# The seam between a scan layer and an attention layer: the last half's output made inside the attention, its matrices folded beside the scan, the last product in four blocks

## The chip, the cores and the metric

The kernel runs on one core of a Trainium2 chip. The metric is the device time of one execution in microseconds (us). Five engines take part, each with its own queue of instructions that it works through in order: TensorE (PE; its weight loads are shown apart as PEld), VectorE (DVE), ScalarE (ACT), GpSimd (POOL) and SyncE (SP), which here only issues DMA transfers. Engines wait for each other by semaphores.

## What is computed

Four images of 32 x 32 positions with 256 channels (4096 rows of 256 numbers, float32) go through two layers. Cut to what matters here:

```python
# layer 0: normalize, project to 512, 3x3 depthwise convolution, gelu, then for every
# batch, channel d and state n (64 of them) a recurrence over the 1024 positions:
h = exp(dt[:, :, None] * A) * h + (dt * x)[:, :, None] * B[:, None, :]
y = einsum('bdn,bn->bd', h, C)
y = layernorm(y + x * D_skip) * g + b
t = src + y @ w_out + b_out
# layer 1: an attention without softmax over the positions of one batch
qkv = layernorm(t) @ W_qkv + b_qkv
q, k = q - mean(q), k - mean(k)          # over channels
k2 = l2norm(k*k / (sum(k*k) + 1e-7), over positions)
q2 = l2norm(q*q / (sum(q*q) + 1e-7), over channels)
t = t + (v + q2 @ (k2^T v) / sqrt(N)) @ W_out + b_out
# then a mixture of 16 experts, two of them for each row
t = t + experts(layernorm(t))
```

The means of q and k over the channels, and the product of v's weights with W_out, depend on the weights alone. The kernel folds them into the weights: it takes off the column means and the row means of W_qkv and multiplies the v part by W_out.

## The kernel before, in words

**The scan.** The recurrence runs over eight units, (batch, half): a half is 512 positions. A unit has 64 states, and a state has four blocks of 128 channels, so a unit has 256 slots. In each slot ScalarE makes one `da` (decay, L695) and one `bx` (scale, L687), PE turns bx (turn, L701), VectorE scans 512 positions (scan, L712). After a state's fourth block POOL multiplies the whole state by C (L719, 128 x 2048), and PE adds the product up, turned, into four PSUM banks y0 to y3 (add_up, L733), nine slots late (LAG). The C row of a state is fetched by SP three states ahead (fetch, L681, four buffers). When a unit is over, close_sum (L746) copies the four banks to `ysb`, two on VectorE and two on ScalarE.

The order of the scan is written out by hand: the loop at L815 walks the slots. Other work is slipped in beside it: `beside(u)` (L753) lists what is due in unit u, as pieces with an engine, a cost and a window of slots; a piece is put in when its slot has come, its gap has passed, its engine has room in the slot (MOST) and, for PE, the single spare bank `bg` is free. In this way the convolution of a later unit, its projections (dt_bc) and the output of the unit before (after_stats, roots_after, after) run beside the scan. In the last two units there is no convolution left to make.

**The output of a unit** (after, L587): per 128 rows, x's rows are fetched (`xr`), b_out is added on POOL, ysb is turned on PE and copied to `yT`, multiplied by w_o (L616), scaled by the row's root and added to xr, and stored in DRAM in `td` (L627). For the last unit nothing is left to hide it beside: it runs alone after the scan (L866 to L871), with its roots made by a logarithm, an exponential and a correction on POOL.

**The attention** (from L925) is not ordered by hand: a scheduler orders each engine's queue when the program is built. It first loads W_qkv, W_out and the biases, and the four batches' rows `t_all` from td (L941, 1 MB each). Then it folds the weights (L945 to L1004): sums by a matmul with ones (L953), means taken off (L958 to L977), v's weights turned and multiplied by W_out (L983 to L994), biases likewise. The loop over the batches (L1018) takes row statistics (statistics, L1006: BN and aggregate on VectorE, a root on ScalarE, a reciprocal), scales the rows to `xh` on ScalarE (L1023), turns them to xhT on PE (L120, copied by VectorE at L1027), and for each of 8 tiles of 128 rows multiplies by the q and k weights (`pqk`, L1037), adds the bias (`qk`, L1042), squares and sums, and multiplies by the folded v weights (`pv`, L1054). The rest of a batch, the routing and the experts (L1326 on) follow.

Of the kernel before, what the change touches and what calls it, by code (L numbers as in the profile page):

```python
# [16 lines left out]
P = 128  # L17
# [16 lines left out]
def conv_ssm_attn_moe_kernel(ctx: ExitStack, tc: tile.TileContext, a: dict, out: bass.AP):  # L34
# [99 lines left out]

    with ExitStack() as l0:
# [3 lines left out]
        scanp = l0.enter_context(tc.tile_pool(name="scan", bufs=2))  # L139
        ps_y = l0.enter_context(tc.tile_pool(name="ps_y", bufs=1, space=PSUM))  # L140
        ps_w = l0.enter_context(tc.tile_pool(name="ps_w", bufs=3, space=PSUM))
# [38 lines left out]
        w_o = load_rows("L0_conv_w_out", DK, C, w0)  # L180
        b_o = load_bcast("L0_conv_b_out", C, w0)
# [33 lines left out]
        for m in range(DK):  # L215
            pad = w0.tile([P, HH + 2, WW + 2], F32, name=f"pad{m}")
            nc.gpsimd.memset(pad, 0.0)
            pads.append(pad)
# [426 lines left out]

        def run(*lists):
            for todo in lists:
                for _, _, _, what, _, _ in todo:
                    what()
# [54 lines left out]
        def scan(s, m):  # L704
            u, n = steps[s]
            b, seg = units[u]
            if m == 0:
                made["h", s] = scanp.tile([P, DK, BANK + 1], F32, name="h", bufs=4)
            if seg == 0 and n == 0 and m == 0:
                last[b] = acts.tile([P, NS, DK], F32, name="last", bufs=1)  # L710
            h = made["h", s]
            nc.vector.tensor_tensor_scan(  # L712
                h[:, m, 1:], made.pop(("da", s, m)), made.pop(("dbx", s, m)),
                0.0 if seg == 0 else last[b][:, n, m : m + 1],
                ALU.mult, ALU.add,
            )
            if m == DK - 1:

                nc.gpsimd.tensor_tensor(  # L719
                    h[:, :, :BANK], h[:, :, 1:], over_middle(made["c", s], DK), ALU.mult  # L720
                )
                if seg + 1 < NHALF:
                    with nc.allow_non_contiguous_dma(reason="one element a partition"):
                        nc.sync.dma_start(out=last[b][:, n, :], in_=h[:, :, BANK])
# [21 lines left out]
        def close_sum(u):  # L746
            t = acts.tile([P, TPB, DN], F32, name="ysb", bufs=1)
            for j in range(TPB):
                eng = nc.scalar.copy if j % 2 else nc.vector.tensor_copy
                eng(t[:, j, :], made["y", u][j])  # L750
            made["ysb", u] = t

        def beside(u):  # L753
# [8 lines left out]
            if v < n:  # L762
                b, half = units[v]
                if u == 0:
                    lists.append([
                        (head(b, 0), (11, 44)), (head(b, 1), (44, 77)), (conv(v), (77, 236)),
                    ])
                elif half == 0:
                    lists.append([(head(b, 1), HEAD1), (conv(v), CONV0)])
                else:  # L770
                    lists.append([(conv(v), CONV1)])
                    if b + 1 < NB:
                        lists[-1].append((head(b + 1, 0), HEAD0))
            if u > 0:
                lists.append([(after_stats(u - 1), STATS)])
# [22 lines left out]
        AFTER = ((14, 110), (112, 245))  # L798

# [66 lines left out]
        alone = True  # L866
        u = len(units) - 1
        run(after_stats(u))
        logs(made["rs"], made["mv"][:, :, 1])
        roots_after(u)  # L870
        run(*after(u, None))  # L871

# [52 lines left out]
    with tc.tile_pool(name="wa", bufs=1) as wa, tc.tile_pool(name="att", bufs=1) as att, \  # L925
            tc.tile_pool(name="sm", bufs=2) as sm, \
            tc.tile_pool(name="ps_b", bufs=2, space=PSUM) as ps_b:
        wqkv = load_rows("L1_attn_W_qkv", CK, 3 * C, wa)
        bqkv = load_bcast("L1_attn_b_qkv", 3 * C, wa)
        bv = load_column("L1_attn_b_qkv", CK, wa, lo=2 * C)  # L930
        wout = load_rows("L1_attn_W_out", CK, C, wa)
        bout = load_bcast("L1_attn_b_out", C, wa)
# [6 lines left out]
        tbs = [t_all[:, b * NT : (b + 1) * NT, :] for b in range(NB)]  # L939
        for b in range(NB):  # L940
            nc.sync.dma_start(out=tbs[b], in_=rows(td, b))  # L941

        wcat = wa.tile([P, CK, 3 * C], F32, name="wcat")  # L945
        wv = wa.tile([P, CK, C], F32, name="wv")
        bcat = wa.tile([P, 3 * C], F32, name="bcat")
        every1 = wa.tile([P, P], F32, name="every1")
        nc.vector.memset(every1, 1.0)
        for n0, n in ((0, 2 * C), (2 * C, C)):  # L950
            ps = ps_b.tile([P, BANK], F32, name="pw", tag="pq", bufs=3)
            for ck in range(CK):
                nc.tensor.matmul(  # L953
                    ps[:, :n], every1, wqkv[:, ck, n0 : n0 + n],
                    start=(ck == 0), stop=(ck == CK - 1),
                )
            for ck in range(CK):
                nc.vector.scalar_tensor_tensor(  # L958
                    wv[:, ck, :] if n0 else wcat[:, ck, :n], ps[:, :n], -1.0 / C,
                    wqkv[:, ck, n0 : n0 + n], ALU.mult, ALU.add,  # L960
                )
        mean = sm.tile([P, CK, 2], F32, name="w_mean")
        for ck in range(CK):
            qk = wcat[:, ck, : 2 * C].rearrange("p (s c) -> p s c", s=2)
            nc.vector.tensor_reduce(mean[:, ck, :], qk, AX.X, ALU.add)
            for s in range(2):
                nc.vector.scalar_tensor_tensor(
                    qk[:, s, :], mean[:, ck, s : s + 1].to_broadcast([P, C]), -1.0 / C,
                    qk[:, s, :], ALU.mult, ALU.add,
                )  # L970
        bmean = sm.tile([P, 2], F32, name="b_mean")
        bqk = bqkv[:, : 2 * C].rearrange("p (s c) -> p s c", s=2)
        nc.vector.tensor_reduce(bmean, bqk, AX.X, ALU.add)
        for s in range(2):
            nc.vector.scalar_tensor_tensor(
                bcat[:, s * C : (s + 1) * C], bmean[:, s : s + 1].to_broadcast([P, C]), -1.0 / C,
                bqk[:, s, :], ALU.mult, ALU.add,  # L977
            )
        wvT = wa.tile([P, CK, C], F32, name="wvT")
        for m in range(CK):  # L980
            ps = ps_b.tile([P, BANK], F32, name="pw", tag="pq", bufs=3)
            for ck in range(CK):
                nc.tensor.transpose(  # L983
                    ps[:, blk(ck, P)], wv[:, ck, blk(m, P)], ident
                )
            nc.scalar.copy(wvT[:, m, :], ps[:, :C])
        for ck in range(CK):
            ps = ps_b.tile([P, BANK], F32, name="pw", tag="pq", bufs=3)
            for m in range(CK):
                nc.tensor.matmul(  # L990
                    ps[:, :C], wvT[:, m, blk(ck, P)], wout[:, m, :],
                    start=(m == 0), stop=(m == CK - 1),
                )
            nc.scalar.copy(wcat[:, ck, 2 * C :], ps[:, :C])  # L994
        bvw = wa.tile([P, CK, P], F32, name="bvw")
        nc.vector.tensor_copy(bvw, over_last(bv, P))
        ps = ps_b.tile([P, BANK], F32, name="pw", tag="pq", bufs=3)
        for m in range(CK):
            nc.tensor.matmul(
                ps[:, :C], bvw[:, m, :], wout[:, m, :], start=(m == 0), stop=(m == CK - 1)  # L1000
            )
        bvo = wa.tile([P, C], F32, name="bvo")
        nc.vector.tensor_copy(bvo, ps[:, :C])
        nc.gpsimd.tensor_tensor(bcat[:, 2 * C :], bvo, bout, ALU.add)  # L1004

        def statistics(tb, tag):  # L1006

            mv = sm.tile([P, NT, 2], F32, name="ln_mv", tag=tag + "mv")
            for i in range(NT):
                st = sm.tile([P, 6], F32, name="ln_st", tag=tag + "st")  # L1010
                nc.vector.bn_stats(st, tb[:, i, :])
                nc.vector.bn_aggr(mv[:, i, :], st)
            rs = sm.tile([P, NT], F32, name="ln_rs", tag=tag + "rs")
# [3 lines left out]

        for b in range(NB):  # L1018
            tb = tbs[b]
            _, rs = statistics(tb, "ln2")  # L1020
            xh = att.tile([P, NT, C], F32, name="xh", bufs=2)
# [12 lines left out]
            for i in range(NT):  # L1034
                pqk = ps_b.tile([P, 2, C], F32, name="pqk", tag="pq", bufs=3)
                for ck in range(CK):
                    nc.tensor.matmul(  # L1037
                        pqk.rearrange("p s c -> p (s c)"), xhT[:, ck, blk(i, P)],
                        wcat[:, ck, : 2 * C], start=(ck == 0), stop=(ck == CK - 1),
# [3 lines left out]
                    qk, pqk, bcat[:, : 2 * C].rearrange("p (s c) -> p s c", s=2), ALU.add  # L1043
# [7 lines left out]
                nc.gpsimd.tensor_tensor(tb[:, i, :], tb[:, i, :], bcat[:, 2 * C :], ALU.add)  # L1051
                pv = ps_b.tile([P, C], F32, name="pv", tag="pq", bufs=3)
                for ck in range(CK):
                    nc.tensor.matmul(  # L1054
                        pv, xhT[:, ck, blk(i, P)], wcat[:, ck, 2 * C :],
# [61 lines left out]
            for ck in range(CK):  # L1117
                pw = ps_b.tile([P, C], F32, name="pkw", tag="po")
                for m in range(CK):
                    nc.tensor.matmul(  # L1120
                        pw, kvT[:, m, blk(ck, P)], wcat[:, m, 2 * C :],
# [355 lines left out]
```

## Time and profile before

| | |
|---|---|
| time, median of 3 runs | 3609.48 us (3608.98 to 3614.11) |
| profiled execution | 3609.15 us |
| its span, first to last instruction | 3607.3 us |
| busy share PE, VectorE, ScalarE, POOL | 90%, 83%, 79%, 69% |
| chain that ended last: ScalarE, PE | 60%, 20% |
| end of the last scan | 2796.5 us |
| first product of the experts | 3141.3 us |

The span stands 1.85 us below the time of the same execution. In the profile, a group row gives line, engine, operation, output and inputs by the program's names, shapes and count, then busy time, the mean of one in ns, and the idle time of that engine just before them with what ended it. A timeline row gives start and length in us, then the same names; in brackets stands how long the engine had been idle and who released it. A row of the waits gives who waited for whom, the sum in us, how often, and the longest.

The units of the scan end (first copy of ysb) at 471.6, 811.9, 1148.2, 1488.5, 1825.1, 2162.3, 2490.6 and 2802.6 us. In the unit from 2162.3 to 2490.6, VectorE is busy for 315.1 us and ScalarE for 326.2; in the last one, to 2802.5, for 303.4 and 302.3.

### The profile page before, as it was taken

How to read it: one execution, taken by the hardware profiler on the slowest of the kernel's cores; microseconds unless marked ns; L12 is line 12 of the kernel's file. 1: busy time of each engine (PE TensorE's matmuls, PEld its weight loads, DVE VectorE, ACT ScalarE, POOL GpSimd, SP SyncE). 2: the span in 40 equal slices, each digit the busy share in tenths (PEclk: the TensorE clock that was granted, in tenths of full speed). 3: DMA queues.
4: the chain of work that ended last, by engine and by line, in shares of the span. 5: the costliest groups of instructions: out<-in, count | busy, mean ns of one | idle time of the engine just before them, and what ended most of it. 6: DMA issues, size and time to landing. Idle time of an engine off the chain costs nothing.

```text
span 3607.3 us, 60573 instructions
## 1 busy us (share of the span) xinstructions
PE 3245.6 (90%) x22292; PEld 2626.9 (73%) x22292; DVE 2981.9 (83%) x3398; ACT 2863.8 (79%) x4748; POOL 2484.2 (69%) x906
## 2 busy tenths in 40 slices
PE   8989999999998998999999989898999788599995
PEld 3678777777777777777777777777777455399985
DVE  5799999999999999999999999999999666622224
ACT  1799999999999999999999999999999244121211
POOL 0489878987897798879878987998888110033331
PEclk9999999999999999999999999999999999699997
DMA  3223222212222122222222122222121200299996
GB/s 101 64 55 76 56 64 65 61 57 58 71 69 60 62 62 61 64 63 66 60 64 64 57 59 54 55 58 57 55 60 55 73 24 12 100 381 325 319 302 236
DMA packets 355165, 334.41 MB, mean 93 GB/s; under 512 B 162081, under 2 KB 241441, under 8 KB 354866
## 3 DMA queue, kind: packets, MB, share of 16 engines
q1 hardware_dynamic: 334834, 306.21, 29.1%
q0 software_dynamic: 7104, 19.41, 1.6%
q10 hardware_dynamic: 12928, 4.89, 0.5%
q8 instruction: 177, 2.90, 0.3%
q14 instruction: 122, 1.00, 0.1%
HBM read 304.21 MB, written 25.69 MB: 91 GB/s over the span
## 4 chain that ended last, share of the span: by engine, by line
ACT 60%; PE 20%; DMA 8%; DVE 7%; issue 2%; POOL 0%; POOLq 0%; DVEq 0%; ACTq 0%; SPq 0%
ACT da L695 28%; ACT bx L687 28%; DMA yd<-yb,dst 6%; PE ps L701 4%; PE y L733 3%; PE p L1377 3%; DVE h L712 3%; PE pqk L1037 2%; PE bg L382 1%; PE pf L1389 1%; DMA xb<-xd,src 1%; PE pv L1054 1%; PE ps L382 1%; PE ps_t L120 1%; ACT L695 1%
## 5 line engine op out<-in xcount | busy, mean ns | idle before, releaser
L719 POOL TENSOR_TENSOR h<-h,cb_n 128x2048 f32<-128x2048 f32 x512 | 2143.6, 4192 | 416.7 <-DVE h L712 328.0
L701 PE MATMUL ps<-ident,bx 128*128 128x128 f32 x8192 | 1323.3, 283 | 197.8 <-DVE h L712 138.0
L687 ACT ACTIVATE bx<-dtxT,bT 128x512 f32<-128x512 f32 x2048 | 1451.5, 709 | 16.5 <-DVE dtxT L534 16.5
L695 ACT ACTIVATE da<-dt,l_conv_a_log_sb 128x512 f32<-128x512 f32 x2048 | 1452.2, 709 | 13.6 <-DVE h L712 13.3
L701 PEld LDWEIGHTS ps<-ident,bx 128*128 128x128 f32 x8192 | 937.2, 142 | 632.8 <-DVE h L712 307.9
L712 DVE TENSOR_TENSOR_SCAN h<-da,last,ps 128x512 f32<-128x512 f32 x1024 | 1231.6, 1263 | 30.3 <-ACT da L695 21.6
L733 PE MATMUL y<-ident,h 128*128 128x128 f32 x8192 | 1246.1, 275 | 5.7 <-POOL h L719 5.6
L712 DVE TENSOR_TENSOR_SCAN h<-da,ps 128x512 f32<-128x512 f32 x1024 | 1189.5, 1207 | 49.4 <-ACT da L695 32.6
L733 PEld LDWEIGHTS y<-ident,h 128*128 128x128 f32 x8192 | 974.5, 143 | 7.8 <-POOL h L719 6.7
L1383 DVE TENSOR_TENSOR hT<-s,p 128x256 f32<-128x256 f32 x148 | 62.4, 421 | 336.4 <-ACT s L1382 336.4
L1377 PE MATMUL p<-xT,w 128*128 128x128 f32 x2368 | 291.6, 277 | 0.5 <-ACT xT L1366 0.5
L1377 PEld LDWEIGHTS p<-xT,w 128*128 128x128 f32 x2368 | 285.1, 194 | 4.8 <-ACT xT L1366 0.9
L1382 ACT ACTIVATE s<-p 128x256 f32<-128x256 f32 x148 | 56.9, 384 | 275.5 <-PE p L1377 275.5
L1397 POOL DMA_INDIRECT yd<-yb,dst x74 | 73.2, 990 | 264.5 <-DMA yd<-yb,dst 185.9
L382 PE MATMUL bg<-pad,dgc 128*128 128x512 f32 x432 | 222.2, 596 | 0.0
L1346 POOL DMA_INDIRECT xb<-xd,src x74 | 72.1, 975 | 132.8 <-DVE dst L1318 108.7
L1389 PE MATMUL pf<-w,hT 128*128 128x256 f32 x592 | 153.3, 382 | 0.1
L1051 POOL TENSOR_TENSOR t_all<-t_all,bcat 128x256 f32<-128x256 f32 x32 | 23.0, 747 | 164.6 <-ACT xh L1023 159.9
L1389 PEld LDWEIGHTS pf<-w,hT 128*128 128x128 f32 x592 | 101.7, 192 | 8.2 <-DVE hT L1383 0.5
L1366 ACT COPY xT<-px 128x256 f32<-128x256 f32 x74 | 27.6, 372 | 77.5 <-PE px L1364 77.5
L382 PEld LDWEIGHTS bg<-pad,dgc 128*128 128x128 f32 x432 | 65.5, 192 | 0.0
L382 PE MATMUL ps<-pad,dgc 128*128 128x512 f32 x144 | 64.0, 605 | 0.7 <-DVE e L487 0.7
(287 smaller groups left out, 2056.5 us busy)
## 6 DMA issues: line engine op xcount, KB each, us to landing
cb_n<-cd SPq DMA_DIRECT2D x512, 256.0 KB, 3.3
w<-in_L_ffn_w_dram SPq DMA_DIRECT2D x222, 512.0 KB, 6.2
dgc<-diags SPq DMA_DIRECT2D x84, 192.0 KB, 3.1
y<-yd SPq DMA_DIRECT2D x8, 1024.0 KB, 9.6
last<-h SPq DMA_DIRECT2D x256, 2.0 KB, 2.9
xr<-in_x_dram SPq DMA_DIRECT2D x32, 128.0 KB, 3.2
td<-xr SPq DMA_DIRECT2D x32, 128.0 KB, 3.3
t_all<-td SPq DMA_DIRECT2D x4, 1024.0 KB, 10.0
```

The source lines that it names most:

```text
L382: nc.tensor.matmul(made["bg"].rearrange("p (h w) -> p h w", w=WW), made["dgc", m * 3 + i][:, j, :], pads[m][:, half * ROWS + i : (half + 1 ...
L687: nc.scalar.activation(t, made["dtxT", u][:, j, :], AF.Copy, scale=made["bT", u][:, j, n : n + 1])
L695: nc.scalar.activation(t, made["dt", u][:, m, :], AF.Exp, scale=A[:, m, n : n + 1])
L701: nc.tensor.transpose(t[:, blk(j, P)], made["bx", s, j][:, blk(m, P)], ident)
L712: nc.vector.tensor_tensor_scan(h[:, m, 1:], made.pop(("da", s, m)), made.pop(("dbx", s, m)), 0.0 if seg == 0 else last[b][:, n, m : m + 1] ...
L719: nc.gpsimd.tensor_tensor(h[:, :, :BANK], h[:, :, 1:], over_middle(made["c", s], DK), ALU.mult)
L733: nc.tensor.matmul(made["y", u][j][:, blk(m, P)], made["h", s][:, m, blk(j, P)], ident, is_transpose=True, start=n == 0 and m == 0, stop=n ...
L1037: nc.tensor.matmul(pqk.rearrange("p s c -> p (s c)"), xhT[:, ck, blk(i, P)], wcat[:, ck, : 2 * C], start=(ck == 0), stop=(ck == CK - 1),)
L1346: nc.gpsimd.indirect_dma_start(t, None, xd[:, :], bass.IndirectOffsetOnAxis(src[:, i : i + 1], 0))
L1377: nc.tensor.matmul(p12[:, j, s, :], on[w, i][:, ck, blk(h + j, P)], on["xT", i][:, ck, :], start=(ck == 0), stop=(ck == CK - 1),)
L1389: nc.tensor.matmul(on["pf", i], on["hT", i][:, hk, :], on["w3", i][:, hk, :], start=(hk == 0), stop=(hk == HK - 1),)
L1397: nc.gpsimd.indirect_dma_start(yd[:, :], bass.IndirectOffsetOnAxis(dst[:, i : i + 1], 0), yb, None)
```

## The change

Five parts:

- The folding of the attention's weights moves from the attention to the scan: `matrices()` is a list of pieces that `beside` puts into the second-to-last unit (u = 6), in slots 20 to 245. The results lie in the memory of the convolution's padded images, which are no longer needed there; a new pool, keep0, holds these, w_o, b_o and ysb beyond layer 0. The six loads that belong to it are issued by SP.
- In the last state of the last unit, POOL multiplies each block of 128 channels by C as soon as it is scanned, in four instructions of 128 x 512 in place of one of 128 x 2048.
- The block that made the last unit's output after the scan is gone. `last_half()` makes it inside the attention, behind the first batch's statistics, with the attention's own `statistics` for the roots, and adds it to x's rows in place in t_all. It is not stored in td.
- The first batch's rows are fetched first, in two halves; x's rows of the last half follow. `load_rest` fetches the other batches' rows after the first batch's reciprocal: VectorE writes one element of each place first, so that the loads wait for it.
- The PSUM pools ps_w and ps_y change places.

```diff
+    keep0 = ctx.enter_context(tc.tile_pool(name="keep0", bufs=1))
+    w_o = keep0.tile([P, DK, C], F32, name="l0_conv_w_out_sb")
+    b_o = keep0.tile([P, C], F32, name="l0_conv_b_out_row")
...
+        ps_w = l0.enter_context(tc.tile_pool(name="ps_w", bufs=3, space=PSUM))
         ps_y = l0.enter_context(tc.tile_pool(name="ps_y", bufs=1, space=PSUM))
-        ps_w = l0.enter_context(tc.tile_pool(name="ps_w", bufs=3, space=PSUM))
...
+            def load():
+                nc.sync.dma_start(out=wqk, in_=w_in[:, :, : 2 * C])
+                nc.sync.dma_start(out=wv, in_=w_in[:, :, 2 * C :])
+                nc.sync.dma_start(
+                    out=wout, in_=a["L1_attn_W_out"].rearrange("(k p) n -> p k n", p=P)
+                )
+                nc.sync.dma_start(out=bqk, in_=b_in[: 2 * C].partition_broadcast(P))
+                nc.sync.dma_start(out=bout, in_=a["L1_attn_b_out"].partition_broadcast(P))
...
+            todo = [
+                piece(1, "SP", 0, load),
+                piece(1, "DVE", 0.2, lambda: nc.vector.memset(ones1, 1.0)),
+            ]
+            for w, n in ((wqk, 2 * C), (wv, C)):
+                for ck in range(CK):
+                    todo.append(piece(
+                        8 if ck == 0 else 1, "PE", 0.88 * n / BANK,
+                        lambda w=w, n=n, ck=ck: sums(w, n, ck), "" if ck else "take",
+                    ))
+                for ck in range(CK):
+                    todo.append(piece(
+                        1 if ck else 3, "DVE", 0.69,
+                        lambda w=w, n=n, ck=ck: off_columns(w, n, ck), "free" if ck else "",
+                    ))
+            for w, m in ((wqk[:, 0, :], mean[:, 0, :]), (wqk[:, 1, :], mean[:, 1, :]), (bqk, bmean)):
+                todo.append(piece(1, "DVE", 0.69, lambda w=w, m=m: rows_of(w, m)))
+                for s in range(2):
+                    todo.append(piece(1, "DVE", 0.42, lambda w=w, m=m, s=s: off_rows(w, m, s)))
...
+            if s == len(steps) - 1:
+                nc.gpsimd.tensor_tensor(h[:, m, :BANK], h[:, m, 1:], made["c", s], ALU.mult)
+            elif m == DK - 1:
-            if m == DK - 1:
...
+            if v == n:
+                lists.append([(matrices(), MATS)])
...
-        alone = True
-        u = len(units) - 1
-        run(after_stats(u))
-        logs(made["rs"], made["mv"][:, :, 1])
-        roots_after(u)
-        run(*after(u, None))
...
+        tbs = [t_all[:, b * NT : (b + 1) * NT, :] for b in range(NB)]
+        for g in range(NHALF):
+            nc.sync.dma_start(
+                out=tbs[0][:, blk(g, TPB), :], in_=rows(td, 0)[:, blk(g, TPB), :]
+            )
+        nc.sync.dma_start(out=tbs[-1][:, TPB:, :], in_=rows(xf, NB - 1)[:, TPB:, :])
+
+        def load_rest(rs):
+            for b in range(1, NB):
+                n = TPB if b == NB - 1 else NT
+                t = tbs[b][:, :n, :]
+                nc.vector.tensor_copy(t[:, :1, :1], rs[:, :1])
+                nc.sync.dma_start(out=t, in_=rows(td, b)[:, :n, :])
...
+        def last_half():
+            ysb = made["ysb", len(units) - 1]
+            _, rs = statistics(ysb, "ln1", TPB)
+            for j in range(TPB):
+                t = tbs[-1][:, TPB + j, :]
+                nc.gpsimd.tensor_tensor(t, t, b_o, ALU.add)
+                ps = ps_b.tile([P, BANK], F32, name="ps_l", tag="po")
+                for m in range(DK):
+                    nc.tensor.transpose(ps[:, blk(m, P)], ysb[:, j, blk(m, P)], ident)
+                yT = sm.tile([P, BANK], F32, name="yT")
+                nc.vector.tensor_copy(yT, ps)
+                po = ps_b.tile([P, C], F32, name="po_l", tag="po")
+                for m in range(DK):
+                    nc.tensor.matmul(
+                        po, yT[:, blk(m, P)], w_o[:, m, :], start=(m == 0), stop=(m == DK - 1)
+                    )
+                nc.vector.scalar_tensor_tensor(
+                    t, po, rs[:, j : j + 1], t, ALU.mult, ALU.add
+                )
...
         for b in range(NB):
             tb = tbs[b]
             _, rs = statistics(tb, "ln2")
+            if b == 0:
+                load_rest(rs)
+                last_half()
```

## The prediction

> **What bounds the kernel now.** I read the page first, then the timeline of the seam between the scan and the attention, then the waits of single stretches. On the page, the shares of the chain and the groups say that the scan (28% + 28% on ScalarE) is set by ScalarE's bx and da activations, and that VectorE's scan stands close behind.
>
> ```profile
> span 3607.3 us, 60573 instructions
> ...
> L695 ACT ACTIVATE da<-dt,l_conv_a_log_sb 128x512 f32<-128x512 f32 x2048 | 1452.2, 709 | 13.6 <-DVE h L712 13.3
> L712 DVE TENSOR_TENSOR_SCAN h<-da,last,ps 128x512 f32<-128x512 f32 x1024 | 1231.6, 1263 | 30.3 <-ACT da L695 21.6
> ```
>
> The change touches the scan's last two units and what follows. The timeline of that seam (start, length, what, idle before it and who ended it):
>
> ```profile
> 2796.65 4.17 POOL L719 TENSOR_TENSOR h<-h,cb_n 128x2048 f32<-128x2048 f32 x1 [0.51 <-POOL h L719]
> ...
> 2802.55 1.29 DVE L750 COPY ysb<-y 128x512 f32<-128x512 f32 x2 [6.03 <-PE y L733]
> ...
> 2812.65 3.45 PE L616 MATMUL ps<-l_conv_w_out_sb,yT 128*128 128x256 f32 x8 [2.80 <-DVE yT L610]
> ...
> 2826.86 5.64 SPq L941 DMA_DIRECT2D t_all<-td  x4
> 2826.98 4.36 PE L953 MATMUL pw<-l_attn_w_qkv_sb,every 128*128 128x512 f32 x8 [4.21 <-issue]
> ...
> 2839.25 1.28 ACT L1014 ACT_TABLE_LOAD   x1 [3.53 <-DVE ln_mv L1012]
> ...
> 2841.56 3.31 ACT L1023 ACTIVATE xh<-t_all,ln_rs 128x256 f32<-128x256 f32 x8 [0.72 <-issue]
> ...
> 2848.87 0.69 DVE L1042 TENSOR_TENSOR qk<-pqk,bcat 128x512 f32<-128x512 f32 x1 [0.17 <-PE pqk L1037]
> ```
>
> The reader is to see a serial road: the last scan ends at 2796.5, the last product (POOL) at 2800.8, the sums are copied out at 2802.6, then the last half's output is made and stored (to 2823.7), weights are loaded and folded (2820 to 2837), t_all is fetched (2826.9), and only at 2841.56 does batch 0 start. From the scan's end to the first qk it is 52.4 us, in which no engine is full. From there PE repeats 2.58 us per tile (the eight qk rows run from 2848.87 to 2866.93).
>
> Waits in the scan's second-to-last unit (2162 to 2491 us), where new work goes:
>
> ```profile
> DVE h L712 <- ACT da L695: 7.9, 4, 3.3
> ...
> ACT da L695 <- DVE h L712: 2.0, 3, 0.7
> ```
>
> ScalarE waits there for VectorE only three times, 2.0 us in all. Pairing each da row with its scan row shows where: VectorE falls up to 7.0 us behind around slots 40 to 55 of 256, catches up at the long activations near slot 90, and is within 0.1 us of ScalarE after that.
>
> [...] 2048 elements take 4192 ns, but 512 (L518, sum_up) take 1276 ns, so four of these are 5.1 us and not 4.2. [...] the trace has 1.28 us, on the road at 2839.25. [...] Here the eight L616 instructions after an idle stretch took 3.45 us, and 1.99 us once warm (2817.55). [...] the four 1 MB loads of t_all landed about 5.5 us after the first issue and then 3.0 us apart.
>
> **The change part by part.** Time is counted as in the trace; T = 2796.5 is the last scan's end. The built order (which fixes each queue and what each wait is for) was read for the rest.
>
> *Preparing the matrices beside the scan* (matrices, MATS) takes the fold off the road. Its instructions stand in unit 6. VectorE gets 0.17 (memset, as L949) + four off_columns (2 x 0.65, 2 x 0.37, from L958: 1.29 and 0.74 a pair) + three reductions (0.63 each, L965) + six off_rows (0.36 each, L967) + two copies of 512 (0.67), bvw 0.30, bvo 0.42: 8.3 us. PE gets about 6 us in a unit that has 299 of 328 busy; POOL one 0.73; SP six loads, 1.4 MB, some 0.4 us of issue each, between C fetches that run three states, 14.7 us, ahead. ScalarE gets nothing. VectorE's part costs only where ScalarE is already held up: in the built order the memset and two off_columns of wqk, 1.5 us, lie at slots 29 to 47, at the peak of the lag; two of 0.37 at slots 72 and 73, where the lag is 3.3 us and has room; the other 6 us come after slot 98, one piece in 8 slots or so, where the lag is 0.1 us and VectorE needs 1.17 against ScalarE's 1.225 a slot. Bounds: 0 (hidden by the 7.9 us for which VectorE waits) and 8.3. I take +1.3.
>
> *Last state's products block by block.* The POOL product before ends at 2796.1. Four blocks at 1.276 end at 2801.3, 0.5 later than the single one; but PE then has 4 matmuls left instead of 16, and the copy needs only the first. From 2800.83 to 2802.55 it was 1.72; now about 0.45. ysb starts at 2801.75, a gain of 0.8. Bounds: 1.3 (blocks at a quarter of 4.19) and 0.4.
>
> *Batch 0's rows alone.* In the built order its two 512 KB loads follow the last C fetch on SP and wait only for the last scan: issue at 2796.6, landed [...] by 2800.3 and 2801.9. x's 512 KB (for the last half) follow, by 2803.4. All are in before VectorE is free at 2803.0 (two ysb copies, 1.29).
>
> *Batch 0's statistics.* Eight tiles at 0.43 (two BN and two aggregates every 0.87 from 2838.36 on), and the built order puts two of ysb's at about 0.70 among them: 4.9 us, to 2807.9. Then table load, root, reciprocal as before, 2.31 us (2839.25 to 2841.56): xh at 2810.3. VectorE's other ysb statistics and the first yT copy, 2.1 us, lie under this. Before it was 2841.56: **31.3 us earlier**.
>
> *Last half's output inside batch 0.* This gives part back. What goes: stores to td and reloads of that half, the Ln and Exp tables, POOL's refinement. SP loses four stores and four loads, two of which stood between the last C fetches; POOL's four t + b_o (0.73 each) wait for x's rows and end by 2806.4, before batch 0 needs POOL. What comes in between xh and the first qk: on PE four transposed groups (0.5) and four groups of L616's kind, the first cold (3.4, as at 2812.65), then 1.99; on VectorE four yT copies (0.67) and four additions (0.48), each waiting for PE and PE for it. PE's queue in the built order: out 0, turn 1, eight transposes of xh (ck = 0), out 1, turn 2, the other eight, out 2, turn 3, half of pqk 0, out 3, the other half. Followed through: out 0 from 2809.9 to 2813.3; xh's eighth activation to 2813.7, its transposes to 2814.9; out 1 and the ck = 1 transposes to 2818.5; out 2 to 2820.4; yT 3 on VectorE at 2821.5; out 3 to 2823.5; second half of pqk 0 to 2824.4. VectorE in front of qk 0 has still six statistics, an addition and a reciprocal: qk 0 at 2825.0, that is 14.7 us after xh, against 7.3 before: **7.4 us given back**.
>
> An added wait lies here. load_rest stamps t_all after the reciprocal, so batch 1's 1 MB is issued at 2810.6 and lands 5.5 us later, at 2816.1. VectorE's first statistic of batch 1 stands behind the second xhT copy (ends about 2816); queued behind it are output additions, yT copies and the ck = 1 copies on which pqk depends. I take 0, since both times agree; ends: -0.5, and +4.5 if landing takes the 10.0 us median of the old four.
>
> *Rest.* The qk loop keeps 14 statistics of batches 2 and 3 (0.43 each), 6 us, with 8 x 1.6 us of its own (qk, addition, reduction by their spacing): 18.8 on VectorE against 18.1 before, so +0.7. Batches 1 to 3, routing and experts keep their instructions and order; their first loads wait for the routing, as before.
>
> Sum: -31.3 (with 0.8 of the product in it) + 7.4 + 0.7 + 1.3 = **-21.9 us**. The profiled execution took 3609.15 us (span 3607.3, 1.85 around it), 0.3 below the median of 3609.48. So 3609.15 - 21.9 = 3587.3; I say 3587.5.
>
> **The rivals.**
> (1) *VectorE becomes the bound of unit 6.* All 8.3 us show, not 1.3: +7.0, 3594.5. For it: the lag of 7 us and VectorE's 315 us busy of 328. Against: units with more VectorE work (328.6 us busy in 1148 to 1488) lasted only as much longer as ScalarE's own work grew.
> (2) *Attention's start is slower*: batch 1's rows late (+4.5) and PE at half rate through the other three output groups (1.5 each, +4.5, partly under the former): +6, 3593.5. For it: PE is left idle in pieces of several us. Against: from xh on it has a matmul every us or two.
> (3) *A slower kernel.* PE stays at half rate into batch 0's qk loop: its matmuls there are 20.6 us at full rate, and in each batch some 54 us busy of 61. Half rate adds half its own length to a PE-bound stretch, so it would have to last 44 us to eat 21.9. At half rate through batch 0 and a half more (90 us) it gives 3587.5 + 45 = 3632. Speaks against it: before, half rate under load lasted 6.8 us at 2840 after an idle stretch of 6 us, then PE ran full. It decides only if the idle pieces go on past qk 0.
> (4) *It doesn't do what it says*: t_all's first load waits for something later than the last scan, 3 to 5 us per stage at most: inside the range.
>
> **How the numbers follow.** Forecast 0.67; (1) 0.14; (2) 0.12; (3) 0.04; the remaining 0.03 for a seam that gains under 7 us. The low end is the forecast's with hidden matrices (-1.3), no extra in the loop (-0.7), early blocks (-0.5), warm out groups (-3): 3582. The high end takes in rivals 1 and 2 with a few us of both: 3597. Within 0.2% (about 7.2 us, what a measurement can tell from no change) is 3602.3 to 3616.7: faster 0.93, same 0.03, slower 0.04.
>
> **What would show it.** Right: last scan at 2797 to 2799; t_all's first issue within 0.1 us of it; ysb near 2802 to 2804; xh 14 us after the scan's end; qk 0 about 28.5 us after it; the loop 18 to 20 us; no wait for DMA over 1 us on VectorE. Wrong: units 6 and 7 longer by over 3 us together (rival 1), a VectorE wait for t_all's rows of several us or out groups of over 3 us each (rival 2), a granted clock at half beyond the first tiles (rival 3).

## The result and the profile after

The changed kernel takes 3601.03 us (median of 20 runs, 3594.13 to 3611.71) against 3613.80 for the kernel before in the same series (3608.98 to 3628.98): a ratio of 0.9963, 95% interval 0.9954 to 0.9972, or 10 to 17 us less. I had predicted 21.9 us less. Of the 13.5 us between the forecast 3587.5 and 3601.0, some 9 are gain that did not come; the rest is the kernel before, which stood 4.6 us higher in this longer series than the 3609.15 I had counted from.

The profiled execution after took 3606.84 us. The page's span and the two groups shown of before:

```profile
span 3605.1 us, 60553 instructions
...
L823 ACT ACTIVATE da<-dt,l_conv_a_log_sb 128x512 f32<-128x512 f32 x2048 | 1467.5, 717 | 23.2 <-DVE h L840 22.4
...
L840 DVE TENSOR_TENSOR_SCAN h<-da,last,ps 128x512 f32<-128x512 f32 x1024 | 1232.3, 1264 | 30.4 <-ACT da L823 20.4
```

ScalarE now waits 22.4 us for VectorE over the scan, 13.3 before. The timeline of the seam, where the last scan ends at 2815.54:

```profile
2815.11 4.60 POOL L846 TENSOR_TENSOR h<-h,cb_n 128x512 f32<-128x512 f32 x4
2815.57 0.92 SPq L1056 DMA_DIRECT2D t_all<-td  x2
...
2820.52 0.67 DVE L880 COPY ysb<-y 128x512 f32<-128x512 f32 x1
...
2826.93 1.28 ACT L1086 ACT_TABLE_LOAD   x1 [5.62 <-issue]
...
2828.75 3.78 PE L1104 MATMUL po_l<-l_conv_w_out_sb,yT 128*128 128x256 f32 x8 [6.19 <-DVE yT L1101]
2828.84 0.51 ACT L1119 ACTIVATE xh<-t_all,ln_rs 128x256 f32<-128x256 f32 x1 [0.31 <-DVE ln_mv L1084]
...
2843.93 0.68 DVE L1138 TENSOR_TENSOR qk<-pqk,brow 128x512 f32<-128x512 f32 x1
```

From the last scan it is 0.03 us to the first load, 4.98 to the sums' copy, 13.3 to xh and 28.4 to the first qk, where I had forecast 0.1, 5.25, 13.8 and 28.5. The lengths of the seam are right; what is missing was lost before it: the first qk is only 4.9 us earlier on the clock of the trace (2848.87 before), though the seam is 24.0 us shorter. The waits of unit 6 (from 2168.15 to 2509.88) answer to the two lines shown of before:

```profile
ACT da L823 <- DVE h L840: 11.9, 10, 3.4
DVE h L840 <- ACT da L823: 4.6, 2, 2.5
```

ScalarE, the engine that sets the scan's pace, is held up for 11.9 us (2.0 before), and the unit lasts 341.7 us in place of 328.2. The lines of VectorE in that unit name the added operation that costs most, the row passes (L699: the row means taken off); second, the same operation before, in the fold behind the scan:

```profile
L699 DVE SCALAR_TENSOR_TENSOR wqk<-w_mean,wqk x4: 1878/2498/4009, 2301.3 to 2343.6; 128x256 f32<-128x256 f32 x4
L699 DVE SCALAR_TENSOR_TENSOR brow<-b_mean,brow x2: 4101/4266/4432, 2366.5 to 2380.1; 128x256 f32<-128x256 f32 x2
```

```profile
L967 DVE SCALAR_TENSOR_TENSOR wcat<-w_mean,wcat x4: 415/418/419, 2833.6 to 2834.6; 128x256 f32<-128x256 f32 x4
```

(Columns: shortest, median, longest in ns, first and last start.) The six row passes take 19.4 us together in the scan; at the price I had used they would be 2.2. Set beside POOL's rows, each ends 0.28 to 0.29 us after a product of POOL (L849) ends, whenever it began. Pairing da with scan rows, VectorE is in the mean 1.0 us behind ScalarE at slots 104 to 111 of the unit and 8.3 us behind at 160 to 167; before, it was 0.05 and 0.15 us there.

The same unit holds a counterpart: the column passes are the same operation on the same engine, but one of their inputs lies in PSUM. Three of the four start while a product of POOL runs, the fourth 0.22 us ahead of one; they take no longer than in the fold before (686 and 414 ns, where POOL stood still):

```profile
L691 DVE SCALAR_TENSOR_TENSOR wqk<-bg,wqk 128x512 f32<-128x512 f32 x2 | 1.3, 667 | 0.0
L691 DVE SCALAR_TENSOR_TENSOR rough<-bg,rough 128x256 f32<-128x256 f32 x2 | 0.8, 400 | 0.0
```

**Theory A**, then: a VectorE operation with both inputs in SBUF (the memory in which the tiles lie; PE's results lie in PSUM) can't run while POOL's product does, and waits for its end. **Theory B**: 18 pieces are too many for these slots, whatever their form.

### The profile page after: what moved, and what is told of

It reads as the page before. It is cut to its first block, busy times and chain, and to the rows that moved or that the text cites. A ratio compares the mean times of both kernels' runs of the same rounds, so it can differ in the third digit from the quotient of the medians.

```text
span 3605.1 us, 60553 instructions
## 1 busy us (share of the span) xinstructions
PE 3242.5 (90%) x22292; PEld 2633.4 (73%) x22292; DVE 2990.5 (83%) x3404; ACT 2865.1 (79%) x4741; POOL 2483.1 (69%) x904
## 5 line engine op out<-in xcount | busy, mean ns | idle before, releaser
L849 POOL TENSOR_TENSOR h<-h,cb_n 128x2048 f32<-128x2048 f32 x511 | 2139.5, 4192 | 434.3 <-DVE h L840 348.0
L823 ACT ACTIVATE da<-dt,l_conv_a_log_sb 128x512 f32<-128x512 f32 x2048 | 1467.5, 717 | 23.2 <-DVE h L840 22.4
L815 ACT ACTIVATE bx<-dtxT,bT 128x512 f32<-128x512 f32 x2048 | 1466.8, 717 | 18.7 <-DVE dtxT L540 17.6
L1147 POOL TENSOR_TENSOR t_all<-t_all,brow 128x256 f32<-128x256 f32 x32 | 22.9, 742 | 171.4 <-ACT xh L1119 171.4
```

Of the source, the lines that this page charges most:

```text
L815: nc.scalar.activation(t, made["dtxT", u][:, j, :], AF.Copy, scale=made["bT", u][:, j, n : n + 1])
L823: nc.scalar.activation(t, made["dt", u][:, m, :], AF.Exp, scale=A[:, m, n : n + 1])
L849: nc.gpsimd.tensor_tensor(h[:, :, :BANK], h[:, :, 1:], over_middle(made["c", s], DK), ALU.mult)
```

## The experiments

The scan's units, the seam and the first batch can be compared from trace to trace; the rest varies with the execution (up to the first scan 129.7 to 134.6 us, the experts' products 421 to 432 us in these traces, with the same instructions). All lengths in us; "qk 0" is the first qk, counted from the last scan's end; "batch" is from there to the first qk of batch 1; the ratio is to the kernel before in the same series (its median is 3613.8 to 3616.7 us in them), with its 95% interval.

| kernel | units 0 to 5 | unit 6 | qk 0 | batch | time | ratio |
|---|---|---|---|---|---|---|
| before | 2032.7 | 328.2 | 52.4 | 60.9 | 3613.8 | |
| changed, first trace | 2035.5 | 341.7 | 28.4 | 62.6 | 3601.0 | 0.9963 (0.9954 to 0.9972) |
| changed, again (e5) | 2034.8 | 342.0 | 28.5 | 62.6 | 3604.3 | 0.9963 (0.9949 to 0.9976) |
| changed, again (e6) | 2034.7 | 340.3 | 27.5 | 61.3 | 3603.7 | 0.9960 (0.9947 to 0.9974) |
| sums in PSUM (e1) | 2032.4 | 329.8 | 27.8 | 61.1 | 3590.8 | 0.9926 (0.9907 to 0.9945) |
| sums in PSUM (e13) | 2032.4 | 329.8 | 27.9 | 61.1 | 3593.7 | 0.9935 (0.9920 to 0.9949) |
| row passes twice (e2) | 2034.7 | 342.6 | 28.5 | 62.6 | 3605.5 | 0.9976 (0.9966 to 0.9987) |
| matrices after the scan (e3) | 2038.5 | 329.4 | 32.6 | 64.1 | 3607.5 | 0.9978 (0.9969 to 0.9987) |
| one last product (e4) | 2035.5 | 332.8 | 28.0 | 61.3 | 3602.3 | 0.9964 (0.9946 to 0.9983) |
| half first (e8) | 2036.0 | 332.6 | 25.3 | 60.6 | 3594.3 | 0.9939 (0.9915 to 0.9962) |
| half in its old place, sums in PSUM (e10) | 2032.4 | 329.7 | 35.2 | 60.9 | 3598.9 | 0.9956 (0.9940 to 0.9972) |
| half first, sums in PSUM (e11) | 2032.7 | 329.3 | 24.7 | 62.6 | 3589.4 | 0.9922 (0.9906 to 0.9938) |
| all rows at once, sums in PSUM (e12) | 2032.4 | 329.8 | 25.5 | 66.2 | 3595.4 | 0.9939 (0.9919 to 0.9958) |
| sums in PSUM, tiles moved 64 bytes (e14) | 2035.6 | 330.4 | 28.9 | 62.6 | 3597.0 | 0.9950 (0.9915 to 0.9986) |
| changed, tiles moved 32 bytes (e15) | 2033.3 | 332.3 | 28.0 | 62.2 | 3591.9 | 0.9936 (0.9909 to 0.9962) |
| before, tiles moved 96 bytes (e16) | 2035.5 | 329.3 | 52.3 | 60.9 | 3616.8 | 1.0006 (0.9998 to 1.0013) |

**The form of the row pass.** The row sums go to the spare PSUM bank. The two small tiles that held them are gone, which also moves the scan's tiles by 64 bytes; what that alone does is measured further down.

```diff
-            def rows_of(w, m):
+            def rows_of(w):
+                m = take()[:, :2]
                 nc.vector.tensor_reduce(m, w.rearrange("p (s c) -> p s c", s=2), AX.X, ALU.add)
-            def off_rows(w, m, s):
+            def off_rows(w, s):
+                m = made["bg"][:, s : s + 1]
                 nc.vector.scalar_tensor_tensor(
-                    w[:, blk(s, C)], m[:, s : s + 1].to_broadcast([P, C]), -1.0 / C,
+                    w[:, blk(s, C)], m.to_broadcast([P, C]), -1.0 / C,
```

> Changed kernel, but the row sums of the matrices are written to PSUM, so that the six row passes (L699 in the changed kernel, 1.9 to 4.4 us each beside POOL's product, 19.4 us together) have one operand in SBUF instead of two; slots, counts and results stay. Theory A (a row pass with both operands in SBUF waits until POOL's running product has ended): each row pass takes about 0.4 us, 2.4 together; unit 6, from the first copy of its predecessor's sums to its own, falls from 341.7 us to 328 to 331, and the time by 10 to 13 us, to about 3588 to 3591. Theory B (VectorE simply has no room for 18 more pieces in these slots, whatever their form): row passes and unit 6 stay as long as they are, the time stays near 3601.

```profile
L699 DVE SCALAR_TENSOR_TENSOR wqk<-bg,wqk x4: 398/400/402, 2291.7 to 2323.0; 128x256 f32<-128x256 f32 x4
L699 DVE SCALAR_TENSOR_TENSOR brow<-bg,brow x2: 397/398/398, 2351.4 to 2352.8; 128x256 f32<-128x256 f32 x2
```

With one input in PSUM the six passes take 2.4 us, at the same busy POOL and in nearly the same slots. Unit 6 is 329.8 us, 1.6 above the kernel before, and the time 3590.8. Theory A holds, B falls, since all 18 pieces are still there: 17.0 us less of row passes make the unit 11.9 shorter; 5 us had fitted into VectorE's slack. With the scan's tiles put back to their place in the changed kernel (e14) the unit is still only 330.4 us, so there it is the form and not the place. Of the 10 us by which the time falls against the changed kernel some 3 are the place, in units 0 to 5 (2032.4 against 2035.5).

**Twice as many.** Every row pass is issued a second time with the factor 0.

> Changed kernel with every row pass of the matrices issued a second time, in a slot of its own, with the factor 0 (it adds nothing to the matrix). Theory A (wait for POOL's product): six more instructions of 2 to 4.4 us, some 19 us, all of it in view since VectorE has no slack left in unit 6: unit 6 goes from 341.7 to 357 to 361 us, the time to about 3617 to 3620. Theory B (each is worth its 0.4 us): 2.5 us more, unit 6 about 344, the time about 3604.

My number for theory A was wrong. Twelve passes took 21.0 us, not 38, and unit 6 342.6 us. All passes over 0.4 us still end 0.28 us after an operation of POOL, but what one costs is what is left of that operation when it comes, and the added passes moved the others to other points of it (0.40, 0.40, 4.02, 1.29, 0.88, 1.98, ... us). The price goes by where each lands, not by the count. The sum alone can't tell A from B here; the single lengths and the former experiment do.

**Chance.** The bias's two passes took 4.43 and 4.10 us in the first trace, and 0.40 and 0.88 in the kernel with one last product, whose unit 6 is built the same.

> The changed kernel once more, nothing edited, for a second trace. In the trace of the whole last product's run the two row passes of the bias took 0.40 and 0.88 us and unit 6 332.8 us, in the changed kernel's first trace 4.43 and 4.10 us and 341.7; the first of the two began 0.02 us ahead of POOL's product there and 0.02 us behind it here. Theory A (the wait runs to the end of POOL's product, so a start a few ns to either side decides): the four passes of wqk take the same 1.9, 2.2, 2.8 and 4.0 us within 0.1, each row pass that waits ends 0.28 us after a product of POOL, and unit 6 is near either 333 or 342. Rival (unit 6's length in the first trace had another cause, such as TensorE's clock): unit 6 varies without the bias's passes.

> The changed kernel a third time, unedited, on the same chip as the three others of this call. Theory A: unit 6 either near 333 (bias's row passes 0.4 and 0.9 us) or near 342 (4.4 and 4.0); against the sums in PSUM 8 to 13 us slower by the medians.

Both repeats show the long case: 4.43 and 3.95, 4.43 and 4.09 us, with unit 6 at 342.0 and 340.3; wqk's four were 1.9, 2.2, 2.8 and 4.0 us each time. Timelines of VectorE (first) and POOL (second) in the changed kernel, then both for the kernel with one last product:

```profile
2366.47 4.43 DVE L699 SCALAR_TENSOR_TENSOR brow<-b_mean,brow 128x256 f32<-128x256 f32 x1
2370.82 2.32 DVE L840 TENSOR_TENSOR_SCAN h<-da,ps 128x512 f32<-128x512 f32 x2
```

```profile
2365.22 1.27 POOL L524 TENSOR_TENSOR e<-e,s 128x512 f32<-128x512 f32 x1
2366.45 4.16 POOL L849 TENSOR_TENSOR h<-h,cb_n 128x2048 f32<-128x2048 f32 x1
```

```profile
2367.89 0.40 DVE L699 SCALAR_TENSOR_TENSOR brow<-b_mean,brow 128x256 f32<-128x256 f32 x1
2368.21 5.66 DVE L840 TENSOR_TENSOR_SCAN h<-da,ps 128x512 f32<-128x512 f32 x5
```

```profile
2366.64 1.28 POOL L524 TENSOR_TENSOR e<-e,s 128x512 f32<-128x512 f32 x1
2367.87 4.47 POOL L847 TENSOR_TENSOR h<-h,cb_n 128x2048 f32<-128x2048 f32 x1
```

The pass meets a gap between two POOL operations. In one case POOL wins and VectorE waits (4.43); in the other VectorE wins and POOL's product takes 4.47 instead of 4.19. I had written that the starts stand on different sides; they don't: in all six traces that have this pass at this point, POOL's recorded start is 15 to 27 ns ahead, and who wins can't be read from it. It makes some 9 us of unit 6 (332.3 to 332.8 in three traces, 340.3 to 342.0 in three), and so may make part of the spread of the changed kernel's times; its own three traces all show the long case.

**Which forms wait.** Nine of each form beside POOL's products, in unit 7 (they compute nothing that is used; the unit grows from 310.9 to 355.3 us, and no time is compared):

> Kernel with the row sums in PSUM, and in its unit 7 36 added VectorE instructions of 256 elements on a scratch tile, five slots apart, four forms in turn: an addition of two tiles in SBUF; an addition of a column (tensor_scalar) to a tile in SBUF; a copy from SBUF to SBUF; a reduction of 512 elements from SBUF. They compute nothing that is used. Theory A [...]: additions, column additions and copies that start during a product of POOL (86% of the time) end 0.15 to 0.3 us after its end, mean 1.5 to 2.5 us; reductions are 0.66 throughout. Rival (only two inputs count): column additions and copies stay at 0.3 to 0.4 us. This tells whether a column addition would have done as well as the sums in PSUM.

```profile
L786 DVE TENSOR_TENSOR trial<-trial x9: 395/2325/3494, 2520.2 to 2799.1; 128x256 f32<-128x256 f32 x9
L787 DVE TENSOR_SCALAR trial<-trial,trial_m x9: 324/927/2208, 2529.0 to 2808.4; 128x256 f32<-128x256 f32 x9
L788 DVE COPY trial<-trial x9: 263/2208/3493, 2537.4 to 2816.0; 128x256 f32<-128x256 f32 x9
L789 DVE TENSOR_REDUCE trial_m<-trial x9: 650/655/662, 2545.4 to 2825.2; 128x2 f32<-128x512 f32 x9
```

Those that start while a POOL operation runs wait: sums of two tiles end 0.28 us after it, column additions and copies 0.15 us after it. Those that start before it don't (0.40, 0.33 and 0.26 us), and the reduction runs through everywhere: 0.65 to 0.66 us for all nine, where the sums and the copies go up to 3.49. So, by these nine (up to 2.21 us), the row pass as a column addition would have waited too. Why these forms wait and the reduction doesn't is not shown. One of the matrices' own pieces was such a copy (bvw, L763 in the changed kernel): 1.22 us, 0.15 us past the end of a product, where my sum had 0.30.

**Parts of the change.** The fold behind the scan, with the rest of the change kept (`run(matrices())` after the slots' loop):

> Changed kernel with the matrices made behind the last scan, ahead of the first batch's statistics, instead of beside the scan: all else of the change stays. Unit 6 returns to 328 us under every theory in which the matrices lengthened it (to 341 only if something else of the change did). In the seam it adds 8 us of VectorE work and the way PE, VectorE, PE in turn: last scan to first qk from 28.4 us to 38 to 46. Theory A: the two nearly cancel, 3601 to 3606, so that moving the matrices beside the scan, as built, has gained next to nothing, and the whole gain is the last half's place. Rival (the matrices beside the scan are cheap and the missing time lies elsewhere): 3611 or more.

The time, 3607.5, lies between the two forecasts (3601 to 3606, and 3611 or more), nearer to theory A's. By the medians moving the matrices as built gained some 6 us, and with the sums in PSUM 17; but 3.0 and 6.1 us of these lie in units 0 to 5, which are longer here. In part that is the place of the tiles (below); in part the scheduler drew the two row passes of the bias into unit 5, where one took 5.87 us, past the ends of two POOL operations to that of a third. The seam grew less than I had thought: qk 0 at 32.6 (38 to 46 expected), which I put down to the last half's output filling the time.

> Kernel with the row sums in PSUM and matrices beside the scan, but the last half's output in its old place, through DRAM ahead of the attention. With the kernel before (neither part), the matrices behind the scan (the last half's part alone, 3607.5 us) and the sums in PSUM (both, 3590.8) this is the fourth corner. In the kernel before the fold began only after the last half's output and lay beside the loads of its rows (issued at 30.3 us after the last scan, first statistic at 38.4). Theory A (each part's time lay partly under the other's; only both together pay): last scan to first qk 44 to 50 us (52.4 before), the time 3607 to 3613, so 1 to 7 us below the kernel before, and 7 + these do not make the 23 of both. Rival (the parts add): 3598, first qk at 36.

Here the theory that each part's time lay under the other's misses its numbers, and the rival's are met: 35.2 and 3598.9. With the rows fetched alone, batch 0's statistics run in the gaps of the old half's output, and only xh waits. In the built order it stands behind the stores and loads of the old half's buffers, whose memory it takes over; the trace doesn't show that (it names a statistic of batch 1), only the wait:

```profile
2818.89 1.28 ACT L1094 ACT_TABLE_LOAD   x1 [5.06 <-issue]
2820.19 0.30 ACT L1094 ACTIVATE ln_rs<-ln_mv,eps 128x8 f32<-128x8 f32 x1
2828.90 3.31 ACT L1126 ACTIVATE xh<-t_all,ln_rs 128x256 f32<-128x256 f32 x8 [8.41 <-DVE ln_st L1091]
```

The times add (some 8 of the one, 16 of the other, 23 to 27 of both), but that is luck. In the seam they don't: the two alone save 19.8 and 17.1 us, both together 24.5, so there much of the one did lie under the other; and the kernel with the matrices behind the scan loses 5.8 us in units 0 to 5 and 3.2 in the batch, which hides this in its time.

> Changed kernel with the last state's product as one instruction of 2048 elements again. From the last scan's end to the first copy of the sums: 4.7 us in the changed kernel, 6.0 in the kernel before. By my step (blocks gain 0.8 us) it is 5.5 to 6.1 here and the rest of the seam moves with it, +0.8 to +1.3 us in the time, which is below what the times can tell. Rival (the copy is held by something else): 4.7 as with blocks.

VectorE's copy of the sums moves to 6.04 us after the last scan, from 4.98 (the 4.7 of the expectation is ScalarE's copy): the blocks gain 1.05 there. Only half of it reaches xh (13.8, 13.3 with blocks), and the first qk doesn't move with it (28.0; the changed kernel's traces have 27.5 to 28.5), so the rest of the seam did not follow as I had expected.

> Changed kernel with the last half's output called ahead of the first batch's statistics instead of behind them. My step (of the output's 15 us, 7.4 are hidden since it runs beside the first batch's activations and transposes): xh moves from 13.3 us after the last scan to 16 to 22, while less stands between xh and the first qk; the first qk from 28.4 to 30 to 36, the time by +2 to +7. Rival (PE's two output groups are the road either way): first qk within 1 us of 28.4.

I expected a loss; the seam gains 2 to 3 us. (The time, 3594.3, is no measure of it: this kernel met the short passes of the bias, 0.40 and 0.89 us.) xh comes at 18.2, as expected, but only 7.2 us lie between it and the first qk (15.1 in the changed kernel), because the output fills the time in which xh can't start, instead of standing between xh's pieces on PE and VectorE.

```diff
-            _, rs = statistics(tb, "ln2")
             if b == 0:
-                load_rest(rs)
                 last_half()
+            _, rs = statistics(tb, "ln2")
+            if b == 0:
+                load_rest(rs)
```

> Both edits together: row sums in PSUM (3590.8 us alone) and the last half's output called ahead of the first batch's statistics (first qk 25.3 us after the last scan, against 28.4 in the changed kernel and 27.8 with the sums in PSUM). Theory A (two separate places, the gains add): unit 6 near 329.8, first qk at 25 to 26, batch 0 to batch 1 at most 61.1; the time 2 to 3 us below that of the sums in PSUM, about 3588. Rival (the output ahead only looked cheaper since its runs met the short unit 6): first qk at 28, no difference between the two.

qk 0 at 24.7 and 3589.4 us, with the batch at 62.6, not the 61.1 I had allowed: the fastest median measured in its series. Against the sums in PSUM alone (3593.7 on the same chip) the gain is 4 us by the medians, with overlapping intervals; it beats the kernel before by 22 to 34 us and the changed kernel (3603.7 there) by 14 by the medians.

> The kernel with the row sums in PSUM once more, for its comparison with the others of this call on one chip. Unit 6 at 329.8 us within 0.5 (no row pass can meet POOL's product, so nothing varies with the start), time 3589 to 3593.

As expected in the stages (329.8 again); the time, 3593.7, is just past the upper edge. The changed kernel on the same chip has 3603.7, 10 us more.

> Kernel with the row sums in PSUM, and the rows of batches 1 to 3 loaded at once, right behind batch 0's rows and x's, instead of behind the first statistics. My step (batch 0's rows are first in the queue and that alone counts; the added wait costs 0): xh at 13.3 us after the last scan as before, batch 0 to batch 1 61.1, the time 3590.8 within 1.5. Rival 2 of the prediction (batch 1's rows come late): the distance of batches 0 and 1, or of the first qk, falls by 1 us or more here. Other rival (3 MB more crowd x's and the gate's loads): first qk later by 1 to 4.

Neither quite: qk 0 comes 2.3 us earlier, but batch 1 begins 5.1 us later counted from there, since batch 1's statistics now stand ahead of and among batch 0's first tiles on VectorE. With the wait that I had priced at 0, batch 1 starts 2.7 us earlier than without it (88.9 against 91.7 us after the last scan); the times (3593.7 against 3595.4) can't tell.

**The place of the tiles.** Units 0 to 5 have the same instructions before and after, but last 2.0 to 2.8 us longer in the changed kernel. Its two tiles of row means push the scan's tiles to 96 bytes above their old place; with the sums in PSUM it is 32. (The PSUM pools that change places do so in all these kernels, those at 2032.4 too, so they are not the cause.)

```diff
+            for k in range(2):
+                pre.tile([P, 2], F32, name=f"spare{k}")
```

> Kernel with the row sums in PSUM and two unused tiles of 32 bytes ahead of the scan's tiles, so that these lie where they lie in the changed kernel (96 bytes above their place before). If the place is the cause: units 0 to 5 together 2035.5 to 2036.0 us as in the changed kernel, and bx at 715 ns. Rival (the row passes or something else of that kernel): 2032.2 to 2032.7 as with the sums in PSUM, bx at 710.

> Changed kernel with one unused tile of 32 bytes more, so that the scan's tiles lie 128 bytes above their place before. If it is the place, and its distance from a multiple of 128 bytes: units 0 to 5 at 2032.7 as before. Rival (not the place): 2035 to 2036. Unit 6 stays near 333 or 341.

> Kernel before with three unused tiles of 32 bytes, so that the scan's tiles lie 96 bytes higher, as in the changed kernel. If it is the place: units 0 to 5 at 2035 to 2036 against 2032.7 before. Rival: 2032.7 within 0.5.

All three go by the place: 2035.6 at 96 bytes, 2033.3 at 128, and 2035.5 for the kernel before at 96. The recorded length of ScalarE's activations goes along: bx takes 715 to 721 ns in the mean in the nine traces with the tiles at 96 bytes, 709 to 713 in the eight others. One of each, the kernel before moved by 96 bytes, then the changed one moved to 128:

```profile
L689 ACT ACTIVATE bx<-dtxT,bT 128x512 f32<-128x512 f32 x2048 | 1475.7, 721 | 17.6 <-DVE dtxT L536 17.6
```

```profile
L816 ACT ACTIVATE bx<-dtxT,bT 128x512 f32<-128x512 f32 x2048 | 1454.8, 711 | 18.8 <-DVE dtxT L540 17.6 <-PE ps L830 1.1
```

This is a companion, not the account: one activation starts some 0.61 us after the other, before the other's record has ended, and 12 ns on each of two activations in 1536 slots would be 37 us, not 2.8. Why 96 costs and 0, 32 and 128 don't is not shown.

## Why the prediction was wrong, step by step

- **What bounds the kernel, and rows alone, statistics.** Right. xh at 13.3 us after the last scan (13.8 forecast, 45.05 before: 31.7 gained, 31.3 forecast).
- **The loads.** In time, though not as priced: the second half of batch 0's rows landed 7.5 us after its issue and x's half 8.4, some 2.5 us later than I had them; only POOL waited for x's half (4.0 us), and its sums were done 4.8 us before they were needed. My landing times were my own estimate; no trace had shown them.
- **The last product.** The four blocks took 4.60 us, not the 5.1 of four times 1276 ns. The blocks gain 1.05 at the copy where I took 0.8, but without them the first qk comes no later, so this term isn't in the seam's gain, and the close agreement of the seam is to that extent luck.
- **Last half inside batch 0.** Right in size: 15.1 us from xh to the first qk (14.7 forecast). That this place is the cheap one was assumed, not tested; ahead of the statistics the same work costs less.
- **The added wait.** Priced at 0; taking it away made batch 1 later, not earlier, so no part of the loss lies here. The three output groups after the first took 1.89 to 1.99 us. Rival 2 is out, and so is rival 3: the clock granted to PE was 1.00 in batch 0's qk loop (2844 to 2862 us).
- **The qk loop.** +0.7 forecast, -0.1 measured (17.98 against 18.06). The whole batch is 1.7 us longer in the first trace and 0.3 in another of the same kernel; in the first, the eight products with the folded v weights that follow the tiles (pkw) took 3.35 us on PE in place of 1.99, in a stretch in which the granted clock was 0.92 (2862 to 2884 us; 1.00 in the same stretch before). That is 1.4 of the 1.7.
- **Matrices beside the scan: the step that failed.** "VectorE's part costs only where ScalarE is already held up ... I take +1.3", with six row passes at 0.36 from L967. That price came from a stretch in which POOL stood still; in unit 6, where POOL is busy for 291.9 of 342 us, a pass waits for POOL's running product to end and costs 0.4 to 4.4 us. The term was +12.1 to +13.8 in three traces of the changed kernel, not +1.3. The slot reasoning itself held (VectorE's lag before was 0.12 us in the mean after slot 98, though up to 0.8 in single slots and not within 0.1): with passes that don't wait, unit 6 grew by 1.6 us. Rival 1 named the place but drew its bound from the same price (all 8.3 us show); a bound needed the wait: six times a whole product of 4.19 is 25 us, and even one pass can take more than that (5.87).
- **Not in the sum at all:** the scan's tiles moved by 96 bytes, +2.0 to +2.8 us.
- **The base.** Three runs put the kernel before at 3609.5; over 20 it is 3613.8.

By the first trace: seam -24.0, unit 6 +13.5, units 0 to 5 +2.8, batch 0 +1.7, the rest of the last unit -0.3, in sum -6.3. The trace of after also began its scan 3.0 us later, with PE's matmuls at 23 to 28 us taking 1.06 us where before they took 0.59 (granted clock 0.50 and 1.00); the kernel before shows that late start too when profiled again with its tiles moved (134.2 against 129.7), so it doesn't take the change to get it. With 1.1 in the rest, this is the -2.2 between the two spans. The medians' -13 is between this and the case in which the bias's passes are lucky (some 9 us less); whether the 20 runs mix the two cases is not shown.

## What to carry to other kernels

Take the price of an operation from a stretch in which the same neighbours run; if the trace has none, put its wait at up to the neighbour's longest instruction (up to 4.43 us here, beside products of 4.19), once in a while more (5.87). For small VectorE work beside a long POOL instruction, keep one input in PSUM: the same arithmetic took 0.40 us here instead of up to 4.43. When work is moved, try it ahead of the chain as well as inside it: here that place was 2 to 3 us cheaper in the seam.

## What was unexpected of the hardware

- A waiting VectorE operation can lose more than one turn: 5.87 us over three POOL operations (matrices after the scan). And VectorE can win, at 0.28 us to POOL (4.47 in place of 4.19, in the kernel with one last product).
- Unused tiles of 96 bytes ahead of the scan's tiles make 1536 slots of the kernel before 2.8 us longer, with ScalarE's activations recorded at 721 ns in place of 709; the kernel's time rises by too little to be told (1.0006).
